# A four-layer graph network on one core: pair 0's layer 2 in another place, matrix quarters summed by adding transfers, and layer 2 of the last two pairs as two sweeps

## The chip, the core and the metric

The kernel runs on one core of one Trainium2 chip. Its engines are TensorE (PE, matrix products), VectorE (DVE), ScalarE (ACT), GpSimd (POOL, here used to issue transfers) and SyncE (SP, which issues transfers only). Each works through its own queue in order and meets the others at semaphores. The metric is the device time of one launch in microseconds, lower is better; of several runs the median counts.

## What is computed

Eight batches of 2048 nodes with 64 features pass through four layers. Every layer ends in a residual sum and a layer norm over the 64 features, and every layer multiplies with the same 2048 x 2048 matrix `adj` (f32):

```python
# layer 0: a graph convolution of order 3 with weights of each node's own
As = [I, A, 2*A@A - I];  w = einsum('nd,dkio->nkio', embedding, weight)
x = layernorm(x + einsum('bnki,nkio->bno', x_g, w) + b)       # x_g: As applied to x
# layer 1: attention over the nodes where adj > 0.5
e = leaky(s1[:, :, None] + s2[:, None, :]);  att = softmax(where(adj > 0.5, e, -9e15))
x = layernorm(x + elu(att @ x))
# layer 2
x = layernorm(x + (adj + I) @ (x @ W.T + b) / deg)
# layer 3: three steps, with row 0 of v replaced at the start
for _ in range(3):
    effects = adj @ v;  v = relu([v, effects] @ W1.T + b1) @ W2.T + b2
x = layernorm(x + v)
```

## The kernel before

**Tiling.** Two batches of 64 features make one *pair* of 128 columns, so there are four pairs, 0 to 3. The state of a pair is a slot `SX0` to `SX3` of 128 partitions x 16 tiles x 128 (1 MB). Three more slots exist: `SA`, `SB` and `SH`. The transposed matrix is read again for each product, in tiles of 256 x 512 f32 (512 KB) by SP (`fetch`, line 234) into a ring of six buffers. A *sweep* (line 1074) multiplies one or two slots with the whole matrix: four column chunks of 512, for each eight tiles, for each tile two matmuls of 128x512 per slot. The sums collect in `acc` (two PSUM banks), and an evicting helper takes them from there.

**Layers.** Layer 0 needs two sweeps per pair (`first_product`, `second_product`) and then, for each of 16 node tiles, eight matmuls into `yp` (line 601) that ACT multiplies with the embedding (line 624) and DVE adds up (636, 638). During the first sweep masks of the matrix are written to DRAM by column, and later by row. Layer 1 is work of DVE and ACT: `scores` (line 700) finds row maxima (line 731), `weights` (798) makes the exponentials in four passes (DVE 809, ACT 817, DVE 822, ACT 825) that PE then multiplies (836), and `finish` (853) normalises; its second `pf` product (870) and the norm after it end a pair's layer 1 (`x2`). Layer 2 is one sweep with `adj + I`, whose diagonal tiles lie in `a_plus_i`; `z_evict` (942), `layer2_tail` (977) and `start_chunk` (1001) take each chunk through a linear map, a norm and a transpose. Layer 3 is three sweeps per pair, each started by a seed product (line 1082) and followed by `h_evict` (951) and `u_chunk` (1024) or, in the last step, `last_chunk` (1044) and `store`.

**The last two pairs.** For pairs 2 and 3 together (`JOINT`), layer 3 takes the matrix in four quarters and the two pairs' columns in four blocks, and forms the product from seven quarter products in place of eight (`joint_layer3`, line 1247). For that it needs four sums and differences of quarters, `s1` to `s4`. These are made in `joint_layer2` (1188): it reads each tile once for both pairs, and `sums` (1170) adds the tiles on DVE (line 1172) and stores them from POOL (1174); diagonal tiles are read a second time without the added identity (`pure`, 1152). The block sums of the two pairs are made by `sums_of_u` (1322), and `keep_m1`, `seed_c22` and `combine` put the quarter products together.

**What sets the order.** `Plan` (line 38) writes the whole order by hand when the program is built: helpers are generators that say which engine they want and what they wait for, with a cost for each step; a number (rank) given to `plan.start` breaks ties. The long chain of sweeps is one such generator (`sweeps`, 1404) with rank 1000, so that anything else that is ready goes in between. PE's order around the change was: all sweeps of layer 0, ending with `second_product(3)`; then for pairs 0 and 1 layer 2 and the three sweeps of layer 3; then the joint part. Tails of layers 2 and 3 run from one queue (`tails`, 971), which begins when layer 0 of the last pair is done.

Of the kernel before, what the change touches and what calls it, by code (L numbers as in the profile page):

```python
# [17 lines left out]
P = 128  # L18
# [125 lines left out]
def resnorm_d4_kernel(  # L144
# [69 lines left out]

    SX = [slots.tile([P, NT, P], F32, name=f"SX{p}") for p in range(NPAIR)]
# [111 lines left out]
    for e in range(2):  # L327
# [20 lines left out]
        for m in ("s1", "s2", "s3", "s4")  # L348
# [84 lines left out]
    def row_tile(t, an, k, done):  # L433
        yield "ACT", [done]
        dg = tiny([P, 1], "dg", 2)
        nc.scalar.activation(an, an, AF.Copy, accum_out=dg)
        done = plan.run("ACT", act(N) + 0.2, done)
        yield "DVE", [done, mr_ring]
        nc.vector.tensor_scalar_add(dg, dg, 1.0)
        nc.vector.reciprocal(rdeg[:, t : t + 1], dg)  # L440
        mk, km = mr_ring.take([P, N], "mr", BF16)
        nc.vector.tensor_scalar(mk, an, THRESHOLD, NEG_INF, ALU.is_le, ALU.mult)
        done = plan.run("DVE", 1.13 + 0.26, done)
        bc_ring.give(k, done)
        nc.gpsimd.dma_start(by_row[t], mk)
        done = plan.dma("DMA", 512, done)
        mr_ring.give(km, done)
        at["by_row", t] = done
        if all(("by_row", i) in at for i in range(NT)):
            at["rows"] = done  # L450
# [125 lines left out]
    def second_pass():  # L576

        for n in range(NPAIR * NCH):
# [32 lines left out]
            xg_ring.give(kx, t_pe)  # L611

# [46 lines left out]
    def layer1(p):  # L659
# [38 lines left out]
        plan.start(10 + p, scores(p, sv, xc, s_rows, done))  # L698

    def scores(p, sv, xc, s_rows, done):  # L700
        s2b = []
        for e in range(2):
            yield "DMA", [bc_ring, done, "rows"]
# [228 lines left out]
    JOINT = (NPAIR - 2, NPAIR - 1)  # L932
    SH_of = {p: SH for p in range(NPAIR)}

    def after_l2(p):
        return SB if p == 0 else SX[p - 1] if p < NPAIR - 1 else SX[0]

    def u_of(p, s):

        return SX[p] if s == 1 else SB if p == NPAIR - 1 else SA  # L940

    def z_evict(p, c, pa, give, done):
# [4 lines left out]
        give(done)  # L947
# [23 lines left out]
    def tails():  # L971
        yield "PE", [("x1", NPAIR - 1)]
# [28 lines left out]
    def start_chunk(p, c, v, done):  # L1001
# [10 lines left out]
        yield "PE", [done, pp_ring]  # L1012
# [11 lines left out]
    def u_chunk(p, c, w, dst, bias, s, done):  # L1024
        yield "PE", [done, pp_ring]
# [48 lines left out]
    def sweep(*products, masks=False):  # L1074

        for c in range(NCH):
            pas = []
            for source, evict, need, before, seed in products:
                yield "PE", [acc_ring, *before(c)]
                pas.append(acc_ring.take([P, CW], "acc"))  # L1080
                if seed:
                    nc.tensor.matmul(  # L1082
                        pas[-1][0], lhsT=seed, rhs=SH[:, tiles(c), :], start=True, stop=False
# [44 lines left out]

    RQ = AQ // 2

    def quarters(k, r):

        return [(k, r), (k, r + RQ), (k + 2, r), (k + 2, r + RQ)]

    def order_of_joint():
        for k in range(2):
            for r in range(RQ):
                order_of_a.extend((c, q, True) for c, q in quarters(k, r))
        for s in range(3):
            for m in ("a11", "a12", "s2", "s3", "a22", "s1", "s4"):  # L1140
                i, j = {"a11": (0, 0), "a12": (0, 1), "a22": (1, 1)}.get(m, (0, 0))
                for k in range(2):
                    for r in range(RQ):
                        if m[0] == "a":
                            order_of_a.append((k + 2 * i, r + RQ * j, False))
# [3 lines left out]
    def pure(k, r):  # L1149

        yield "SP", [("group", k, r), *([xg_ring] if len(xg_ring.freed) > 1 else [NEVER])]
        got = []
        for c, q in (quarters(k, r)[i] for i in (0, 3)):
            t, kt = xg_ring.take([P, 2, CW], "pure")
            nc.sync.dma_start(t, tile_of_adj(c, q))
            got.append((t, kt, plan.dma("SP", 512, xg_ring.t)))
        return got

    def sums(k, r, taken):

        tiles4 = [(t, kt, got) for t, kt, got, _ in taken]
        own = {}
        if r // 2 == k:
            own = dict(zip((0, 3), (yield from pure(k, r))))
        a11, a12, a21, a22 = ((own.get(i) or tiles4[i])[0] for i in range(4))
        ready = [(own.get(i) or tiles4[i])[2] for i in range(4)]

        def out_of(m, a, b, op, *after):
            yield "DVE", [bc_ring, *after]
            t, kt = bc_ring.take([P, 2, HALF], m)  # L1170
            t = t.rearrange("p a b -> p (a b)")[:, 0 : 2 * CW].rearrange("p (t n) -> p t n", n=CW)
            nc.vector.tensor_tensor(t, a, b, op)
            done = plan.run("DVE", dve(2 * CW), *after)
            nc.gpsimd.dma_start(sum_tiles[m][k, r], t)  # L1174
            bc_ring.give(kt, plan.dma("DMA", 512, done))
            return t, done

        s3, d3 = yield from out_of("s3", a11, a21, ALU.subtract, ready[0], ready[2])
        s1, d1 = yield from out_of("s1", a21, a22, ALU.add, ready[2], ready[3])
        s2, d2 = yield from out_of("s2", s1, a11, ALU.subtract, d1)  # L1180
        s4, d4 = yield from out_of("s4", a12, s2, ALU.subtract, d2)
        for (_, kt, _, free), d in zip(taken, (d2, d4, d1, d1)):
            a_ring.give(kt, max(free, d))
        for _, kt, _ in own.values():
            xg_ring.give(kt, d2)
        refill()

    def joint_layer2():
        p, o = JOINT
        at["group", 0, 0] = 0.0  # L1190
        for k in range(2):
            pas = {}
            for r in range(RQ):
                taken = []
                for i, (c, q) in enumerate(quarters(k, r)):
                    n = next(used)
                    if r == 0 and i in (0, 2):
                        if i == 0:
                            yield "PE", [po_ring, ("x2", p), ("x2", o)]
                            t2, kp = po_ring.take([P, 2, CW], "po")  # L1200
                            pas[c] = [(t2[:, e, :], kp) for e in range(2)]
                        else:
                            pas[c] = []
                            for e in range(2):
                                yield "PE", [acc_ring]
                                pas[c].append(acc_ring.take([P, CW], "acc"))
                    for e, pair in enumerate(JOINT):
                        yield "PE", [("a", n)]
                        t, kt = a_tiles[n]
                        for b in range(2):  # L1210
                            m = 2 * q + b
                            nc.tensor.matmul(
                                pas[c][e][0],
                                lhsT=SX[pair][:, m, :],
                                rhs=t[:, b, :],
                                start=(r == 0 and i in (0, 2) and b == 0),
                                stop=(r == RQ - 1 and i in (1, 3) and b == 1),
                            )
                        done = plan.run("PE", mm(CW, 2), ("a", n))
                        if r == RQ - 1 and i in (1, 3):  # L1220
                            if i == 3:
                                give = lambda t, kk=pas[c][e][1]: acc_ring.give(kk, t)
                            else:
                                give = give_half(pas[c][e][1])
                            plan.start(1, z_evict(pair, c, pas[c][e][0], give, done))
                    del a_tiles[n]
                    taken.append((t, kt, at["a", n], done))
                    if i == 0:
                        nxt = (k, r + 1) if r + 1 < RQ else (k + 1, 0)
                        at[("group", *nxt)] = plan.free["PE"]  # L1230
                    spent[0] += 1
                plan.start(5, sums(k, r, taken))
                refill()

    halves_left = {}

    def give_half(kp):
        def give(t):
            left, last = halves_left.pop(kp, (2, 0.0))
            if left == 1:  # L1240
                po_ring.give(kp, max(t, last))
            else:
                halves_left[kp] = (1, max(t, last))

        return give

    def joint_layer3():
        p, o = JOINT
        U, _ = e_ring.take([P, 2, HALF], "u23")
        T12, _ = e_ring.take([P, 2, HALF], "t12")  # L1250
        T34, _ = e_ring.take([P, 2, HALF], "t34")
        T = [
            t[:, i, :].rearrange("p (t n) -> p t n", n=P) for t in (T12, T34) for i in range(2)
        ]
        for s in range(3):
            up, uo = u_of(p, s), u_of(o, s)
            B11, B21, B12, B22 = up[:, 0:8], up[:, 8:16], uo[:, 0:8], uo[:, 8:16]
            plan.start(0, sums_of_u(s, T, B11, B21, B12, B22))
            u = lambda pair, half: lambda k: ("u", pair, s, 2 * half + k)
            t = lambda i: lambda k: ("t", s, i, k)  # L1260
            seed = gv if s else w31v
            held = {}

            for m, B, need, evict, seeded in (
                ("m1", B11, u(p, 0), None, None),
                ("m2", B21, u(p, 1), None, (p, 0)),
                ("m6", T[1], t(1), "u2", None),
                ("m7", T[2], t(2), "u3", None),
# [209 lines left out]
```

## Time and profile before

| what | before |
|---|---|
| median of 3 runs | 2132.62 us (2131.99 to 2137.06) |
| the profiled execution | 2133.99 us |
| its span | 2132.2 us |
| granted TensorE clock, mean | 0.994 |
| PE, matmuls busy | 2067.3 us (97%) |
| DVE busy | 1496.4 us (70%) |
| ACT busy | 974.9 us (46%) |
| POOL busy | 213.0 us (10%) |
| moved by transfers | 495.85 MB, 233 GB/s on average |

The profile is one execution, taken by the hardware. A row of the timeline gives the start and the length in us, the engine, the line, the operation, what it writes and reads, and the count; the time in brackets is how long the engine stood idle before it, and what ended that. Matmuls of f32 with 512 columns appear as two records each, so that x16 stands for eight matmuls. A row of the windows table gives a stretch of the span with the busy time in it, the granted clock, the mean busy share of the 16 DMA engines and the rate.

### The profile page before, as it was taken

The page shows a single profiled execution, that of the slowest core. Times are in us where ns is not written, and L with a number is a line of the kernel's source. Part 1 is how long each engine was busy: PE and PEld are TensorE (multiplying, and loading weights), DVE is VectorE, ACT ScalarE, POOL GpSimd, SP SyncE. Part 2 cuts the span into 40 slices and gives each one's busy share as a digit, 9 for nine tenths or more (in the row PEclk, how much of TensorE's full clock was granted, in tenths as well). Part 3 has the DMA queues.
Part 4 walks back from the last instruction along what each step waited for, and adds up shares of the span by engine and source line. Part 5 has one row for each costly group of instructions (what it writes and reads, how often), then busy time and mean ns, then how long its engine had stood idle before and what let it go on. Part 6 is the DMA issues. An engine that isn't in the chain of part 4 may idle for free. (4 is left out here: it accounts for less than half of the span.)

```text
span 2132.2 us, 19037 instructions
## 1 busy us (share of the span) xinstructions
PE 2067.3 (97%) x6325; PEld 914.9 (43%) x6325; DVE 1496.4 (70%) x1908; ACT 974.9 (46%) x1794; POOL 213.0 (10%) x374
## 2 busy tenths in 40 slices
PE   8999999999999999999798999989999999999998
PEld 3444444433433443433343453443444444444444
DVE  2226647998799999789998979999796455120214
ACT  0025424567776566777624857336575012000002
POOL 2310000100110100000010101011010110000000
PEclk9999999999999999999899999999999999999999
DMA  9799835634443465554388778897776777878785
GB/s 303 267 333 345 306 105 209 218 122 136 138 137 131 159 238 169 170 178 150 124 309 299 254 267 285 279 339 239 264 236 234 290 255 273 280 254 281 251 288 188
DMA packets 208740, 495.85 MB, mean 233 GB/s; under 512 B 20274, under 2 KB 28594, under 8 KB 204530
## 3 DMA queue, kind: packets, MB, share of 16 engines
q1 hardware_dynamic: 165058, 347.62, 48.0%
q0 software_dynamic: 39360, 144.92, 19.7%
q10 hardware_dynamic: 4224, 2.10, 0.4%
q8 instruction: 50, 0.82, 0.2%
q14 instruction: 48, 0.39, 0.1%
HBM read 446.14 MB, written 46.33 MB: 231 GB/s over the span
## 5 line engine op out<-in xcount | busy, mean ns | idle before, releaser
L1093 PE MATMUL acc<-a,SX 128*128 128x512 f32 x1024 | 465.8, 598 | 9.6 <-DMA SX<-in_x 6.6
L1093 PE MATMUL acc<-a,SA 128*128 128x512 f32 x768 | 348.6, 596 | 13.1 <-DMA a<-in_adj_t 12.4
L817 ACT ACTIVATE e<-e,sv 128x1024 f32<-128x1024 f32 x256 | 280.1, 1154 | 114.4 <-DVE e L809 110.6
L731 DVE CUSTOM_DVE_ANT_0 junk<-s2b,mr 128x2048 bf16<-128x2048 f32 x128 | 292.7, 2287 | 5.2 <-DMA mr<-by_row 3.9
L624 ACT ACTIVATE terms<-yp,emb_sb 128x128 f32<-128x128 f32 x896 | 243.5, 400 | 113.6 <-PE yp L601 113.3
L1093 PEld LDWEIGHTS acc<-a,SX 128*128 128x128 f32 x1024 | 190.3, 191 | 242.2 <-issue 229.6
L822 DVE TENSOR_TENSOR e<-e,mb 128x2048 f32<-128x2048 f32 x128 | 290.0, 2286 | 6.0 <-ACT e L817 5.4
L809 DVE TENSOR_TENSOR e<-s1b,mk 128x2048 f32<-128x2048 f32 x128 | 289.1, 2286 | 6.5 <-PE po L836 4.0
L825 ACT ACTIVATE e<-e 128x2048 f32<-128x2048 f32 x128 | 245.0, 1928 | 67.5 <-DVE e L822 67.2
L601 PE MATMUL yp<-SH,xgT 128*128 128x512 f32 x512 | 246.9, 607 | 3.3 <-ACT sv L358 3.3
L836 PE MATMUL po<-e,SX 128*64 128x512 f32 x1024 | 235.4, 602 | 3.1 <-ACT e L825 3.1
L1093 PEld LDWEIGHTS acc<-a,SA 128*128 128x128 f32 x768 | 140.9, 190 | 186.0 <-issue 166.0
L1299 PE MATMUL acc<-a,t 128*128 128x512 f32 x384 | 168.7, 592 | 0.0
L636 DVE TENSOR_TENSOR terms<-terms 128x512 f32<-128x512 f32 (+1 forms) x176 | 130.0, 738 | 42.2 <-ACT terms L624 38.2
L601 PEld LDWEIGHTS yp<-SH,xgT 128*128 128x128 f32 x512 | 90.9, 189 | 145.7 <-issue 137.6
L836 PEld LDWEIGHTS po<-e,SX 128*64 128x64 f32 x1024 | 68.1, 137 | 155.8 <-issue 133.7
L601 PE MATMUL yp<-SH,y2T 64*128 64x512 f32 x512 | 128.3, 617 | 0.0
L804 POOL DMA_DIRECT2D mk<-by_col x128 | 69.0, 540 | 546.7 <-DVE e L809 452.1
L1093 PE MATMUL acc<-a,SB 128*128 128x512 f32 x256 | 118.3, 595 | 0.0
L1299 PEld LDWEIGHTS acc<-a,t 128*128 128x128 f32 x384 | 72.0, 190 | 86.1 <-issue 86.1
L601 PEld LDWEIGHTS yp<-SH,y2T 64*128 64x128 f32 x512 | 43.6, 186 | 79.9 <-issue 76.4
L1093 PEld LDWEIGHTS acc<-a,SB 128*128 128x128 f32 x256 | 47.2, 190 | 57.3 <-issue 57.3
(225 smaller groups left out, 1677.7 us busy)
## 6 DMA issues: line engine op xcount, KB each, us to landing
a<-in_adj_t SPq DMA_DIRECT2D x496, 512.0 KB, 5.5
a<-s SPq DMA_DIRECT2D x96, 512.0 KB, 4.5
mr<-by_row POOLq DMA_DIRECT2D x64, 512.0 KB, 5.9
mk<-by_col POOLq DMA_DIRECT2D x128, 256.0 KB, 5.0
an<-in_adj SPq DMA_DIRECT2D x16, 1024.0 KB, 10.7
s<-s POOLq DMA_DIRECT2D x32, 512.0 KB, 5.0
a<-a_plus_i SPq DMA_DIRECT2D x24, 512.0 KB, 5.0
by_col<-mk POOLq DMA_DIRECT2D x32, 256.0 KB, 5.8
```

What stands on the lines that cost most here:

```text
L601: nc.tensor.matmul(yp[:, e, :], lhsT=y2T[rows, cs] if k2 else xg[:, e, cs], rhs=(wk2 if k2 else w01)[rows, hs], start=(k2 == h), stop=(k2 ...
L624: nc.scalar.activation(batches(terms[0][:, dd, :]), term, AF.Copy, scale=weight)
L636: nc.vector.tensor_tensor(a, a, b, ALU.add)
L731: nc.vector.tensor_tensor_reduce(out=junk, in0=s2b[e][0], in1=masks[t][0], scale=1.0, scalar=LOWEST, op0=ALU.add, op1=ALU.max, accum_out=m ...
L804: nc.gpsimd.dma_start(mk, by_col[jt // 2][:, jt % 2, h * HALF : (h + 1) * HALF])
L809: nc.vector.tensor_tensor(e, s1b[0], mk.unsqueeze(1).to_broadcast([P, 2, HALF]), ALU.add)
L817: nc.scalar.activation(e[:, i, :], e[:, i, :], AF.Prelu, bias=sv[:, 2 + i, jt : jt + 1], alpha=ALPHA)
L822: nc.vector.tensor_tensor(e, e, mb[0], ALU.add)
L825: nc.scalar.activation(e, e, AF.Exp)
L836: nc.tensor.matmul(po[i * C : (i + 1) * C, f, :], lhsT=SX[p][:, t, i * C : (i + 1) * C], rhs=e[:, i, f * CW : (f + 1) * CW], start=(t == 0 ...
L1093: nc.tensor.matmul(pa, lhsT=source[:, m, :], rhs=t[:, i, :], start=(m == 0 and not seed), stop=(m == NT - 1),)
L1299: nc.tensor.matmul(pa, lhsT=B[:, 2 * r + b, :], rhs=at_[:, b, :], start=(r == 0 and b == 0 and not go_on), stop=(r == RQ - 1 and b == 1), ...
```

## The change

It has three parts, and buffers move to other slots with them.

1. Layer 2 of pair 0 is swept ahead of layer 0's last pass (`second_product(3)`). For that, pair 0 uses other slots: its transposed state goes into `SX0` (as soon as the sweep has used it, "x1 used"), its layer-2 result into `SA`, its u into `SB` (after the last pass, "y1 used") and `SH` (after layer 0's weights, "w0 used"). Tails no longer wait for layer 0 of the last pair. `scores` of pair 0 gets rank 1.2 in place of 10 and no longer waits until all row masks are written; the other pairs' get 9.5 + p.
2. The four sums of quarters are made by 64 transfers from DRAM to DRAM, issued by POOL: for each of 4 x 8 tiles one copy and one that adds to it. They are due every 14 us from 320 us of the plan on. Block sums and the putting together of the seven products are reordered to suit the new sums.
3. `joint_layer2` and what belonged to it go. Pairs 2 and 3 get one sweep of layer 2 each, pair 2 first.

```diff
-        plan.start(10 + p, scores(p, sv, xc, s_rows, done))
+        plan.start(1.2 if p == 0 else 9.5 + p, scores(p, sv, xc, s_rows, done))
...
-            yield "DMA", [bc_ring, done, "rows"]
+            yield "DMA", [bc_ring, done]
...
-    JOINT = (NPAIR - 2, NPAIR - 1)
-    SH_of = {p: SH for p in range(NPAIR)}
+    JOINT = (NPAIR - 1, NPAIR - 2)
+    SH_of = {p: SH if p else SX[0] for p in range(NPAIR)}
...
-        return SB if p == 0 else SX[p - 1] if p < NPAIR - 1 else SX[0]
+        return SA if p == 0 else SX[p - 1] if p < NPAIR - 1 else SX[0]
...
-        return SX[p] if s == 1 else SB if p == NPAIR - 1 else SA
+        if s == 1:
+            return SX[p] if p else SH
+        return SB if p in (0, 1, NPAIR - 1) else SA
...
     def tails():
-        yield "PE", [("x1", NPAIR - 1)]
...
-        yield "PE", [done, pp_ring]
+        yield "PE", [done, pp_ring, *(["x1 used"] if p == 0 else [])]
...
+        room = {0: ["y1 used"], 1: ["w0 used"]}.get(s, []) if p == 0 else []
+        yield "PE", [done, pp_ring, *room]
...
+    def sums_of_a():
+        n = itertools.count()
+        for m, a, b in (
+            ("sa", "a12", "a22"),
+            ("sb", "a11", "a12"),
+            ("sc", "sa", "a11"),
+            ("sd", "sc", "a21"),
+        ):
+            for x in (a, b):
+                for k, r in sum_tiles[m]:
...
+                    yield "DMA", [320.0 + 14.0 * next(n), *before]
+                    nc.gpsimd.dma_start(
+                        sum_tiles[m][k, r], part, **({"accum_op": ALU.add} if x == b else {})
+                    )
+                    done = plan.dma("DMA", 900 if x == b else 512) + 1.0
...
-            for m in ("a11", "a12", "s2", "s3", "a22", "s1", "s4"):
+            for m in ("sb", "a11", "sc", "sd", "a21", "a22", "sa"):
...
+            def keep(s, k, pa, done):
+                yield "ACT", [done]
+                nc.scalar.copy(half(X, k), pa)
+            def x_of(s, k, pa, ka, done):
+                nc.vector.tensor_tensor(half(X, k), pa, half(X, k), ALU.subtract)
+            def z_and_v(s, k, pa, ka, done):
+                nc.vector.tensor_tensor(half(Z, k), half(X, k), pa, ALU.subtract)
+                seeded(p, 2 + k, pa, False)
+                nc.vector.tensor_tensor(half(V, k), pa, half(X, k), ALU.subtract)
...
             products = [second_product(p)]
             if 0 < p < NPAIR - 1:
                 products.append(first_product(p + 1))
+            if p == NPAIR - 1:
+                yield from sweep(layer2_product(0))
+                at["x1 used"] = 0.0
             yield from sweep(*products)
+        at["y1 used"] = 0.0
         for p in range(NPAIR - 2):
-            yield from sweep(layer2_product(p))
+            if p:
+                yield from sweep(layer2_product(p))
             for s in range(3):
                 yield from sweep(layer3_product(p, s))
+        yield from sweep(layer2_product(NPAIR - 2))
...
-        yield from joint_layer2()
+        yield from sweep(layer2_product(NPAIR - 1))
         yield from joint_layer3()
...
     plan.start(1, rows_of_adj())
+    plan.start(1, sums_of_a())
     plan.start(1, stacks())
```

## The prediction

> **What bounds the kernel now.** I read the page first for the totals, then the timeline of PE for every wait it has, then the windows table for the transfers beside it.
>
> ```profile
> span 2132.2 us, 19037 instructions
> PE 2067.3 (97%) x6325; PEld 914.9 (43%) x6325; DVE 1496.4 (70%) x1908; ACT 974.9 (46%) x1794; POOL 213.0 (10%) x374
> DMA  9799835634443465554388778897776777878785
> ```
>
> PE is busy 2067.3 of 2132.2 us, so all that an edit can win without removing matmuls is the 64.9 us in which PE stands still. The timeline of PE shows where they are; an entry in brackets is the idle time before the row and what ended it. The two groups that this change touches:
>
> ```profile
> 1005.82 7.13 PE L1093 MATMUL acc<-a,SX 128*128 128x512 f32 x16 [3.07 <-ACT z L945]
> ...
> 1026.55 1.94 PE L836 MATMUL po<-e,SX 128*64 128x512 f32 x8 [1.08 <-ACT e L825]
> ...
> 1033.36 1.13 PE L981 MATMUL ps_emb<-w2bd,z 128*128 128x128 f32 x8 [2.89 <-DVE SB L990]
> 1035.12 2.04 PE L981 MATMUL ps_emb<-w2bd,z 128*128 128x128 f32 x8 [0.64 <-DVE SB L990]
> 1044.58 0.48 PE L1015 MATMUL ps_vT<-ident,v 128*128 128x128 f32 x1 [7.42 <-DVE v L1007]
> ...
> 1120.43 1.98 PE L1093 MATMUL acc<-a,SA 128*128 128x512 f32 x4 [1.24 <-DMA a<-in_adj_t]
> 1124.71 1.98 PE L1093 MATMUL acc<-a,SA 128*128 128x512 f32 x4 [2.30 <-DMA a<-in_adj_t]
> 1128.37 3.70 PE L1093 MATMUL acc<-a,SA 128*128 128x512 f32 x8 [1.68 <-DMA a<-in_adj_t]
> ...
> 1723.24 0.66 PE L1015 MATMUL ps_vT<-ident,SX 128*128 128x128 f32 x4 [1.59 <-DVE SX L510]
> 1727.28 0.63 PE L1015 MATMUL ps_vT<-ident,SX 128*128 128x128 f32 x4 [1.54 <-DVE SX L510]
> ```
>
> Group one is pair 0's layer 2: its tail (linear map, norm, transpose) runs on DVE and ACT, layer 0 and the sweeps have nothing left for PE, and it waits 3.07 + 1.08 + 2.89 + 0.64 + 7.42 = 15.1 us. Group two is the same tail for the two last pairs at once; with its smaller entries (0.66, 0.68, 0.67, 0.67, 0.31, 0.35, 1.33, 0.88) it comes to 8.7 us between 1687 and 1797. Between them lie 5.2 us for adjacency tiles at 1120. The rest is not touched: 6.6 at the start, 6.4 up to 300, 2.5 up to 1000, 3.0 near 1150, 6.6 near 1404 to 1430, 10.1 at the end.
>
> The windows table shows how much transfer PE stands beside it (time, PE busy with count, clock, share of the 16 DMA engines, GB/s):
>
> ```profile
> 1110.00:1160.00 50.00, 41.76 (x120) 1.00 0.92 339
> 1240.00:1330.00 90.00, 90.00 (x293) 1.00 0.84 293
> 1400.00:1440.00 40.00, 33.35 (x96) 1.00 0.99 355
> ```
>
> At a share of 0.84 PE never waits; at 0.92 and 0.99 it does. So the bound is PE's own work, and DMA is what can open holes in it.
>
> **Part 1: PE's work itself.** Layer 2 of the last pairs goes from 32 tiles used twice to two sweeps of 32: 128 matmuls both times. The seven quarter products and their seeds are 112 and 8 per step both times. PE's 2067.3 us stay.
>
> **Part 2: pair 0's layer 2 moved ahead of the last pass.** In the changed order its 64 matmuls stand right behind the second pf of pair 0 and three layer-0 tiles (yp; a fourth stands just ahead of that pf), and its tail lies beside the last pass of layer 0 (64 matmuls of 0.86 us and 16 yp tiles of 5.1), which doesn't need it. The 15.1 us go. What is late next is the input of the moved sweep, x2 of pair 0:
>
> ```profile
> 749.65 1.05 PE L870 MATMUL pf<-back,poT 128*128 128x130 f32 x8
> ...
> 773.05 0.69 DVE L510 TENSOR_TENSOR SX<-SX,ln_r 128x512 f32<-128x512 f32 x1
> ```
>
> Before, that norm ends at 773.7 with DVE never idle from 734.0. The changed order has some 2.9 us less on DVE in this stretch (the sum of its rows), so about 770.8. PE's order up to the first pf is the same; from there (731.2) to the sweep it has 34.5 us of work, so it arrives at 765.7 and waits 5 us; the wait is the sweep's first matmul, and all of PE's queue stands behind it. From below, 0, if DVE drops more; from above 12, since the four yp tiles now stand back to back and each needs 16 x 0.400 = 6.4 us of ACT (row L624) for 5.1 of PE, with two buffers. I take 6, near the DVE row. In the sweep itself PE has only po to fill, and po waits for weights from DVE, four passes of 2.29 us per eight matmuls with scores between; in the trace such waits total 3.1 us. Between 0 and 8, taken as 1.5.
>
> The DMA waits of 5.2 us at 1120 arose where pair 0's first layer-3 sweep ran bare, at 0.86 us a matmul, beside two 1 MB broadcasts. In the new order that sweep is mixed with yp tiles, and reads half as fast. I take 4 of 5.2 as gone (0 to 5.2).
>
> **Part 3: the last pairs apart.** Pair 2's tail now lies under pair 3's sweep, pair 3's under the first four quarter products, which need only pair 2's u (27 us by 32 matmuls of 0.86). The 8.7 us go, 1 stays for short waits as in the row at 1404 (0.44 to 0.67). The cover is the 55 us sweep; without it the 8.7 would return. The price is 32 more tiles: 64 in about 125 us are 268 GB/s, and PE stood 276 without a wait:
>
> ```profile
> 1800.00:1900.00 100.00, 100.00 (x275) 47.67 (x274) 16.40 (x26) 5.57 (x8) 0.00 (x0) 1.00 0.82 276
> ```
>
> So 0. DVE's 32 adds of 1.22 us (39 us), 32 stores and 8 second loads fall away after 1650, where DVE is under 60% busy: 0. Two more sums of u per step and one combine less per half are about 4 us of DVE in all, at 17% busy: 0. The bank that is kept for two products waits for a DVE add of 0.69 us under 6.9 us of matmuls: 0.
>
> **Part 4: the sums by transfers.** 64 transfers of 512 KB on POOL's queue, due every 14 us from 320 on: 32 copies and 32 that add. Their issue is 64 x 0.54 to 0.74 us on a POOL that is 10% busy; behind them stand the mask loads (mr, mk), three buffers deep, and DVE waits for those. For a plain 512 KB the queue table gives 144.92 MB for 19.7% of 16 engines' span, so 1.52 us of all engines. No adding transfer is in the trace. POOL's 10% alone would say that the whole costs nothing. The Trainium skill speaks against that (DMA: Bandwidth & Descriptors, "Issuing engines are not separate DMA queues"): transfers from POOL run on the same 16 engines as SP's. The rows at 0.92 and 0.99 bear it out, and what decides is where the 64 fall. Up to about 770 the share is 0.37 to 0.64, and there they are hidden. In the moved sweep (0.83 by the same mix later, in pair 1's) it is mostly copies: 0.83 + 1.52/14 = 0.94, just at the edge. The last 8 adds fall into pair 0's layer-3 steps at 0.84, where 14 us leave 0.16 x 14 = 2.2 us. If an add costs like the copy row, 0 is lost. The Trainium skill (Collectives: The Full Stack, "The bandwidth ceiling: the fold count and why AG ≠ RS ≠ AR") has an add read two sources and run at half a copy's rate: an estimated 3.0 us, 0.8 over, times 8 = 7. No run here shows which. I take 3.5 of 0 to 7; a gain is excluded, since the traffic is additional.
>
> **The sum.** 2134.0 (the profiled execution: span 2132.2 and 1.8 around it) - 15.1 - 8.7 - 4.0 + 6.0 + 1.5 + 1.0 + 3.5 = 2118.2. The median of the runs lies 1.4 under the profiled execution, so 2117.
>
> **Rivals.** *Better covered*: x2 arrives in time and the adds cost no more than copies; 2117 - 6 - 3.5 - 1.5 = 2106. For it: DVE ran 39 us there without a pause and its order is free to favour the norm. Against: ACT's 6.4 us per yp tile. *Given back at the moved sweep*: the wait for x2 takes 12, po 8, nothing is won at 1120, the adds cost 7: 2117 + 6 + 6.5 + 4 + 3.5 = 2137 at most, 2129 if only the first two hit. For it: DVE is 84 to 98% busy from 700 on, and PE's queue is in order. *Slower, by the adds*: one mechanism, the adding transfer at several times a copy. It decides from where 8 x (T - 2.2) outweighs the 15.8 us won and 6.4 more, T = 5.0 us, 3.3 copies. At T = 6 the last 8 cost 30 us, and the other 24 hold mask loads in the same queue beyond their slack of some 3.5 us (three buffers of 4.7 us, less one in use, against 5.9 us to landing), of which I count 6 on PE: 2117 + 30 + 6 - 3.5 = 2150. Against it: most adds fall in half-idle stretches, and rule and row both say 1.5 to 3. *That it doesn't do what it says* would be pair 0's sweep behind the last pass; the changed order shows it ahead.
>
> **How the numbers follow.** Forecast 0.52, better covered 0.20, given back 0.16, slower 0.12. A measurement of this kernel tells about 0.3% (6.4 us) from no change. Faster (below 2126) holds the first two and a little of the third: 0.74; the rest of the third is "same", 0.14; slower 0.12. The range: down to 2103, just under "better covered"; up to 2134, the middle of "given back", leaving out its end and "slower".
>
> **What would show it.** Right: on PE's timeline no wait over 1 us at ps_emb or ps_vT of pair 0, nor between layer 2 and the quarter products; one wait of about 6 us before the moved sweep, ended by DVE SX L509; PE busy 2065 to 2070; DMA share near 0.95 in the moved sweep and in pair 0's layer 3. Wrong: PE rows there ended by DMA a<-in_adj_t beyond 10 us in total (adds dear), or DVE idle for mr or mk, or po waiting for ACT e L825 beyond 10 us.

## The result, and the profile after

The changed kernel took 2118.22 us (median of 4 runs, 2112.12 to 2120.24), the kernel before beside it 2132.3 us. The ratio is 0.9917 [0.9898, 0.9935], 0.8% faster. The profiled execution of after, 2112.12 us, is the quickest of its four; a second profile of the same kernel, called *after again* below, has a span of 2119.3 us and stands for the median better. Where the two differ, both are given.

The head of the page of after, and the digits of DMA:

```profile
span 2110.3 us, 19036 instructions
PE 2064.0 (98%) x6325; PEld 914.9 (43%) x6325; DVE 1462.1 (69%) x1879; ACT 980.7 (46%) x1791; POOL 253.5 (12%) x406
DMA  9799837775456578788659979788776777778885
```

The span is 21.9 us shorter with the same 6325 matmul records. PE stands still for 46.3 us in place of 64.9; the other 3.3 us are PE's own busy time, which the prediction had taken as fixed (the last section shows what moves it between executions). The timeline of PE in after, with its larger waits behind 300 us (time, length, ..., idle before and what ended it):

```profile
474.38 1.94 PE L836 MATMUL po<-e,SX 128*64 128x512 f32 x8 [1.35 <-ACT e L825]
477.98 0.63 PE L671 MATMUL ps_xT<-ident,SX 128*128 128x128 f32 x4 [1.66 <-DVE SX L509]
...
688.61 0.66 PE L563 MATMUL ps_xg<-ident,SX 128*128 128x128 f32 x4 [3.49 <-ACT terms L624]
...
757.89 0.66 PE L530 MATMUL ps_y<-ident,y1T 128*128 128x128 f32 x4 [1.38 <-ACT terms L624]
...
777.53 15.62 PE L1097 MATMUL acc<-a,SX 128*128 128x512 f32 x36
...
1123.60 1.98 PE L1097 MATMUL acc<-a,SH 128*128 128x512 f32 x4 [1.26 <-DMA a<-in_adj_t]
1127.98 1.98 PE L1097 MATMUL acc<-a,SH 128*128 128x512 f32 x4 [2.40 <-DMA a<-in_adj_t]
1130.99 5.42 PE L1097 MATMUL acc<-a,SH 128*128 128x512 f32 x12 [1.03 <-DMA a<-in_adj_t]
...
1426.60 3.46 PE L1097 MATMUL acc<-a,SB 128*128 128x512 f32 x4 [1.98 <-DMA a<-in_adj_t]
```

Groups one and two are gone, without a rest. The moved sweep starts at 777.53 with no wait. The waits for adjacency tiles near 1120 are still there. And there are waits that before did not have, at 474 to 478 and 677 to 689. The windows of after (PE busy, clock, DMA share, GB/s) at the moved sweep, at 1120, at pair 0's later layer-3 sweeps and in the joint part:

```profile
770.00:850.00 80.00, 79.14 (x245) 1.00 0.78 271
1110.00:1140.00 30.00, 24.97 (x75) 1.00 1.05 339
1240.00:1330.00 90.00, 90.00 (x310) 1.00 0.90 319
1800.00:1900.00 100.00, 100.00 (x276) 1.00 0.80 266
```

At 0.90 PE does not wait; at 1.05 it does. (A share near 1 is not enough by itself: *every7* below passes 1110 to 1140 at 1.02 with PE busy for all 30 us.) The moved sweep shows 0.78, not the 0.95 foretold.

### The profile page after: what moved, and what is told of

It is laid out like the page before. It is cut to its first block, busy times and chain, and to the rows that moved or that the text cites. A ratio compares the mean times of both kernels' runs of the same rounds, so it can differ in the third digit from the quotient of the medians.

```text
span 2110.3 us, 19036 instructions
## 1 busy us (share of the span) xinstructions
PE 2064.0 (98%) x6325; PEld 914.9 (43%) x6325; DVE 1462.1 (69%) x1879; ACT 980.7 (46%) x1791; POOL 253.5 (12%) x406
## 4 chain that ended last, share of the span: by engine, by line
PE 61%; issue 24%; DVE 8%; DMA 3%; ACT 2%; POOL 0%; SPq 0%; POOLq 0%; ACTq 0%; DVEq 0%
PE acc L1097 35%; PE yp L600 12%; PE po L836 10%; DVE junk L731 3%; DMA a<-in_adj_t 2%; DVE terms L636 2%; DVE e L822 1%; DVE e L809 1%; PE ps_u L1032 1%; ACT terms L624 1%; PE acc L1086 1%; DMA an<-in_adj 1%; ACT e L817 1%; PE pf L870 1%; PE ps_sv L681 0%
## 5 line engine op out<-in xcount | busy, mean ns | idle before, releaser
L1097 PE MATMUL acc<-a,SX 128*128 128x512 f32 x1152 | 519.7, 597 | 6.5 <-DMA SX<-in_x 6.5
L1097 PE MATMUL acc<-a,SB 128*128 128x512 f32 x768 | 352.0, 598 | 4.8 <-DMA a<-in_adj_t 4.1
L1097 PEld LDWEIGHTS acc<-a,SX 128*128 128x128 f32 x1152 | 214.6, 191 | 266.0 <-issue 258.1
L1097 PEld LDWEIGHTS acc<-a,SB 128*128 128x128 f32 x768 | 140.8, 190 | 178.5 <-issue 168.1
L636 DVE TENSOR_TENSOR terms<-terms 128x512 f32<-128x512 f32 (+1 forms) x176 | 129.9, 738 | 49.7 <-ACT terms L624 45.5
L1097 PE MATMUL acc<-a,SA 128*128 128x512 f32 x256 | 119.5, 600 | 2.5 <-DMA a<-in_adj_t 2.5
L1210 PE MATMUL acc<-a,t 128*128 128x512 f32 x192 | 85.4, 592 | 0.0
L490 ACT ACTIVATE ln_sq<-SX 128x512 f32<-128x512 f32 x48 | 30.6, 638 | 94.0 <-DVE SX L995 38.9
L718 POOL DMA_DIRECT2D mr<-by_row x64 | 34.8, 549 | 315.0 <-DVE mx L731 268.8
## 6 DMA issues: line engine op xcount, KB each, us to landing
an<-in_adj SPq DMA_DIRECT2D x16, 1024.0 KB, 10.6
```

The lines of the kernel that those rows point to most:

```text
L636: nc.vector.tensor_tensor(a, a, b, ALU.add)
L1097: nc.tensor.matmul(pa, lhsT=source[:, m, :], rhs=t[:, i, :], start=(m == 0 and not seed), stop=(m == NT - 1),)
L1210: nc.tensor.matmul(pa, lhsT=B[:, 2 * r + b, :], rhs=at_[:, b, :], start=(start and r == 0 and b == 0), stop=(r == RQ - 1 and b == 1), skip ...
```

## The experiments

The theory after this profile: the two groups were worth what the waits said, the sums are nearly hidden, and the new early waits are the price. The rivals: the adding transfers eat a good part of the gain; or one part brings the whole of it. The kernels came in three batches of four: move_only to no_sums; joint_no_sums, old_ranks, every7 and after again; and the last four. The kernel before beside them had medians of 2134.9, 2134.8 and 2136.0 us, so kernels of different batches are compared by their ratios. The table gives for each the median, the ratio to the kernel before on the same chip, and from its one profile PE's busy time and the waits that PE's timeline shows, by stretch.

| kernel | median us | ratio [95%] | PE busy | waits 300 to 775 | 775 to 1000 | 1000 to 1160 | 1380 to 1450 | 1600 to 1820 |
|---|---|---|---|---|---|---|---|---|
| before | 2132.3 | 1 | 2067.3 | 2.8 | 0.2 | 23.3 | 6.6 | 8.7 |
| after | 2118.2 | 0.9917 [0.9898, 0.9935] | 2064.0 | 10.7 | 0.0 | 5.0 | 6.1 | 0.0 |
| after again | 2117.9 | 0.9917 [0.9902, 0.9931] | 2071.7 | 9.8 | 0.8 | 4.5 | 7.0 | 0.0 |
| move_only | 2130.1 | 0.9975 [0.9966, 0.9984] | 2071.2 | 4.9 | 7.1 | 0.9 | 8.3 | 11.8 |
| joint_only | 2133.2 | 0.9996 [0.9985, 1.0006] | 2070.7 | 0.0 | 3.6 | 25.0 | 4.7 | 0.0 |
| adds_as_copies | 2113.7 | 0.9901 [0.9887, 0.9916] | 2067.2 | 10.7 | 0.0 | 2.5 | 6.1 | 0.0 |
| no_sums | 2115.9 | 0.9913 [0.9900, 0.9926] | 2068.6 | 4.8 | 7.2 | 0.8 | 6.9 | 0.0 |
| joint_no_sums | 2125.3 | 0.9955 [0.9943, 0.9968] | 2066.8 | 2.8 | 0.2 | 23.2 | 5.2 | 0.0 |
| old_ranks | 2101.2 | 0.9845 [0.9830, 0.9860] | 2062.4 | 1.7 | 0.0 | 2.9 | 9.0 | 0.0 |
| every7 | 2114.4 | 0.9905 [0.9890, 0.9919] | 2066.6 | 5.9 | 3.2 | 0.0 | 13.6 | 0.0 |
| move_old_ranks | 2125.3 | 0.9945 [0.9932, 0.9958] | 2072.0 | 5.4 | 0.6 | 0.8 | 7.7 | 15.5 |
| before_new_rank | 2139.9 | 1.0018 [1.0011, 1.0026] | 2077.3 | 2.9 | 0.0 | 6.4 | 7.5 | 23.7 |
| old_ranks_every7 | 2112.8 | 0.9891 [0.9878, 0.9904] | 2067.7 | 1.3 | 2.5 | 7.8 | 7.1 | 0.0 |
| old_ranks_every10 | 2105.4 | 0.9853 [0.9840, 0.9866] | 2064.3 | 1.7 | 1.1 | 4.6 | 8.2 | 0.0 |

### One part at a time

*move_only* is before with pair 0's layer 2 moved, its slots and the new rank; *joint_only* is after with pair 0 where it was, in its old slots and with the old ranks.

```diff
 move_only, from before:
+            if p == NPAIR - 1:
+                yield from sweep(layer2_product(0))
+                at["x1 used"] = 0.0
             yield from sweep(*products)
...
-        plan.start(10 + p, scores(p, sv, xc, s_rows, done))
+        plan.start(1.2 if p == 0 else 9.5 + p, scores(p, sv, xc, s_rows, done))
 joint_only, from after: the same lines back, the sums and the two sweeps kept
```

> Pair 0's layer 2 moved ahead, with its slots and the scores' ranks, while the last two pairs keep their shared sweep and the sums on DVE. Theory M (each part removes its own waits and pays its own price): the 15.1 us at ps_emb and ps_vT of pair 0 go, 3 to 8 us come back as waits for ACT and DVE before the moved sweep, so 2121 us (2117 to 2125), and the 8.7 us between 1687 and 1797 of before are still there. Theory S (the scores' new ranks cost, the transfers don't): new waits of some 8 us between 470 and 770, as in the changed kernel, show here too. Theory R (the sums' transfers cost): no such waits before 700 here, and 2117 or less.

> The sums by adding transfers, the new order of the seven products and two separate sweeps for the last pairs, while pair 0's layer 2 stays behind the last pass, with the old slots and ranks. Theory M: the 8.7 us near the last pairs' layer 2 go, the 15.1 us of pair 0 stay, the transfers cost 0 to 4, so 2126 us (2123 to 2129). Theory R: the transfers cost 8 us or more, through loads of masks and of adjacency tiles that come late, so 2132 or above, no gain.

Each part removes its group (the 15.1 us at 1000 to 1090 in the one, the 8.7 us of the last pairs in the other), and yet they bring 0.25% and nothing that the measurement tells from zero; together 0.83%. So each part alone pays its gain back elsewhere. Where joint_only pays is on PE's timeline, in pair 0's layer-3 sweeps:

```profile
1121.29 1.99 PE L1095 MATMUL acc<-a,SA 128*128 128x512 f32 x4 [1.21 <-DMA a<-in_adj_t]
1126.16 2.41 PE L1095 MATMUL acc<-a,SA 128*128 128x512 f32 x4 [2.88 <-DMA a<-in_adj_t]
1129.99 6.13 PE L1095 MATMUL acc<-a,SA 128*128 128x512 f32 x8 [1.42 <-DMA a<-in_adj_t]
...
1145.30 1.98 PE L1095 MATMUL acc<-a,SX 128*128 128x512 f32 x4 [1.99 <-DMA a<-in_adj_t]
1149.27 1.13 PE L1095 MATMUL acc<-a,SX 128*128 128x512 f32 x2 [1.98 <-DMA a<-in_adj_t]
```

Over the whole span it waits 19.1 us for adjacency tiles (before 13.1), 13.8 of them between 1100 and 1300 (before 5.2). Four adds are issued right there, at 1105.9, 1119.6, 1132.7 and 1137.1. They are the obvious suspect.

### The sums

*adds_as_copies* lets the 32 adding transfers copy, *no_sums* and *joint_no_sums* leave all 64 out and read plain quarters (from after and from joint_only).

```diff
 adds_as_copies:
-    sum_tiles[m][k, r], part, **({"accum_op": ALU.add} if x == b else {})
+    sum_tiles[m][k, r], part, **{}
 no_sums, joint_no_sums:
-    plan.start(1, sums_of_a())
...
-            src = sum_tiles[c][q]
+            src = tile_of_adj(*q)
```

> The changed kernel with the 32 adding transfers as plain copies of the same bytes to the same place: the addition of the second quarter is left out, so the products of the last two pairs in layer 3 are other numbers. The order of every queue is that of the changed kernel. If an add costs like a copy: within 1 us of the changed kernel (2118). If it costs twice a copy, as I sized it: 2 to 4 us less, with the waits for adjacency tiles at 1120 shorter. Rival (adds several times a copy): 8 us less or more. POOL's issue of an add falls from 1.1 us to 0.7.

> The changed kernel without any of the 64 transfers: in place of the four sums, plain quarters of the matrix are read, so the products of the last two pairs in layer 3 are other numbers; the number of tiles read is the same. Theory M with transfers that are nearly hidden: 2113 to 2116, since 3.5 us were counted for them. Theory R: 2108 or less, and the waits between 470 and 700 and those for tiles at 1120 are gone. Theory S: the waits between 470 and 700 stay.

> Parts 2 and 3 as in the kernel joint_only (pair 0's layer 2 behind layer 0's last pass, last pairs' layer 2 as two sweeps), but the 64 summing transfers are left out and the seven products read plain quarters, so the sums are missing from the result. Theory: alone, the joint part won its 8.7 us and gave them back as waits for adjacency tiles (19.1 us against 12.4 before), because the last sums fell beside pair 0's layer-3 sweeps that had no yp tiles among them. Then without the transfers: waits for adjacency tiles back to 12 us or less, group two still gone, group one still there, time 2134.9 - 8 = 2126 to 2128, a ratio of 0.996 to 0.997. Rival: the transfers are innocent and the pair of sweeps itself costs what it wins (its order or a slower clock): ratio 0.9985 to 1.0005 as in joint_only.

What an add costs can be read from the queue table (packets, MB, share of 16 engines' span), first after, then adds_as_copies:

```profile
q0 software_dynamic: 46272, 161.70, 25.0%
```

```profile
q0 software_dynamic: 42176, 161.70, 22.4%
```

The same bytes take 0.250 x 2110.3 = 527.6 us in place of 0.224 x 2109.6 = 472.6 us of all engines: 55 us for 32 adds, 1.72 us each on top of the copy's 1.52 (the 64 copies against no_sums' 17.7% give 1.54). An add thus costs about 3.2 us where the prediction's estimate was 3.0. On the time, adds as copies are some 3.4 us quicker (0.9901 against 0.9917), but the intervals of the ratios overlap. The same order without any sum is not to be had: with the transfers away the plan writes another order (a wait of 4.57 us at 789.51 that move_only has too and after has not), so that no_sums, at 0.9913, says only that the sums do not cost much.

joint_no_sums against joint_only shows a clear difference: 0.9955 against 0.9996, intervals apart, 8 to 9 us, with 5.1 us of waits for adjacency tiles between 1100 and 1300 in place of 13.8. The windows of joint_only and of joint_no_sums at pair 0's first layer-3 sweeps:

```profile
1110.00:1160.00 50.00, 38.92 (x100) 0.93 1.01 334
```

```profile
1110.00:1160.00 50.00, 41.86 (x120) 1.00 0.93 337
```

So without the sums the joint part wins its group two (9.6 us by joint_no_sums), and with them it gives it back. That the transfers do this, and not the other order that comes with them (joint_no_sums has before's waits again up to 1160), is argued from the four adds beside the waits; joint_only with its adds as copies was not run. In after the first layer-3 sweep of pair 0 has yp tiles among it, and 5.0 us of such waits are left of the 13.8. That is one half of why the parts bring more together than apart.

### The rank of scores

The waits at 474 to 478 and at 677 to 689 belong to no part of the prediction's sum. *old_ranks* restores the old ranks and the wait for the row masks. Of this edit only one number counts: with 10 + p for pairs 1 to 3, or with the wait, the program that the plan writes is the same as after's byte for byte, so all of the difference comes from pair 0's 1.2 in place of 10:

```diff
-        plan.start(1.2 if p == 0 else 9.5 + p, scores(p, sv, xc, s_rows, done))
+        plan.start(10 + p, scores(p, sv, xc, s_rows, done))
...
-            yield "DMA", [bc_ring, done]
+            yield "DMA", [bc_ring, done, *(("by_row", i) for i in range(NT))]
```

> The changed kernel with the old ranks of scores (10 + p for every pair) and the old wait for all row masks. It tells whether the new short waits of about 8 us in all between 470 and 690 us come from pair 0's scores being preferred. If the ranks make them: those waits fall to some 2.5 us as before, but x2 of pair 0 comes later, so the wait at the moved sweep grows; time between 2112 and 2118. If the early rank is what makes x2 punctual: the moved sweep waits 10 us or more at its first matmuls and the time is 2122 to 2130. If the order hardly changes: 2117 to 2119 and the same short waits.

It is the quickest kernel of the study, below all three cases of the expectation: 2101.2 us, 0.9845 [0.983, 0.986], 17 us under after again, which ran beside it. The early waits are gone but for one of 1.68 us at 749, as its windows with PE's busy time show (first old_ranks, then after):

```profile
475.00:500.00 25.00, 25.00 (x80) 1.00 0.67 176
675.00:700.00 25.00, 25.00 (x81) 1.00 0.60 156
```

```profile
475.00:500.00 25.00, 23.12 (x86) 1.00 0.46 113
675.00:700.00 25.00, 20.42 (x68) 0.93 0.59 159
```

I had feared that without the early rank the moved sweep would wait for x2. It does not: it starts at 768.82, 8.7 us sooner than in after, with no wait. What PE stood for at 688.61 in after was the multiplication of a yp tile on ACT, behind three passes of weights (the timeline of ACT in after):

```profile
679.90 1.91 ACT L825 ACTIVATE e<-e 128x2048 f32<-128x2048 f32 x1 [2.52 <-DVE e L822]
682.10 4.39 ACT L817 ACTIVATE e<-e,sv 128x1024 f32<-128x1024 f32 x4 [0.29 <-DVE e L809]
686.40 2.16 ACT L624 ACTIVATE terms<-yp,emb_sb 128x128 f32<-128x128 f32 x8
```

ACT itself had waited 2.52 us for DVE. The rank thus shifts work between DVE's and ACT's queues, and PE pays where layer-1 passes fall ahead of layer 0's. The early waits need the sums in the plan as well: between 300 and 700 us the kernels with the new rank but without sums (move_only, no_sums, before_new_rank) have 2.9 us, like before (2.8), and joint_only, with sums and the old rank, has none. The cost of the adds is not the reason: as copies in the same order they leave the 7.8 us as they are. That points to the order. Two further kernels put the rank on and off elsewhere: *move_old_ranks* is move_only with the old rank, *before_new_rank* is before with the new rank alone.

> The kernel move_only with the old ranks of scores: only pair 0's layer 2 moves, with its slots. If the new rank is what ate the gain of the move in move_only (2130 us, where the 15.1 us of group one were gone): the waits near 476, 687, 753 and 791 us are gone and the time is 2113 to 2118, a ratio of 0.990 to 0.992. If the move itself is worth little, whatever the rank: 2126 to 2131. Whether the last pairs' waits of 8 us near 1698 to 1793 stay: both say yes.

> The kernel before with one edit, the new rank of scores (1.2 for pair 0, 9.5 + p for the others). If the rank by itself makes the short waits between 470 and 790 us and slows the clock behind them: 10 to 17 us slower than before, 2145 to 2152, a ratio of 1.004 to 1.008, and PE waits over 1 us near 475, 680 and 690. If it hurts only together with the moved sweep: 0.998 to 1.002. If an earlier x2 helps pair 0's layer 2 where it stood: a ratio under 0.998.

The rank costs in each of the three comparisons, in two of them less than expected: 0.9975 against 0.9945 for the move alone, 0.9917 against 0.9845 for the whole, and 1.0018 [1.0011, 1.0026] for before, which lies in the range of the case that it hurts only together with the moved sweep. The place differs. In before_new_rank group one is gone too (2.0 us left of 15.1), and 23.7 us of waits stand at 1600 to 1820 instead, 12 of them for the last pair's layer 1. move_old_ranks (2125.3 us) lies between its two cases, and neither names what it shows, a new wait in the old joint layer 2:

```profile
1645.91 3.37 PE L1215 MATMUL po<-a,SX 128*128 128x512 f32 x4 [4.26 <-DVE SX L510]
1679.91 8.59 PE L1215 MATMUL acc<-a,SX 128*128 128x512 f32 x16 [3.16 <-DMA a<-in_adj_t]
```

PE, ahead by the move, comes to the joint layer 2 before x2 of pair 3 is ready: a sweep for both pairs at once needs both inputs at its start, while two sweeps need the second one 55 us later. That is the other half of the gain from both parts together. With the old ranks throughout, the four kernels are 1, 0.9945 (move), 0.9996 (joint), 0.9845 (both): parts 0.6% in sum, both 1.55%, 20 us more. In the one profile of each the spans give 2132.2 - 2125.9 - 2130.5 + 2100.8 = -23.4 us. The waits on PE's timeline make up 56.2 - 45.2 - 49.7 + 28.5 = -10.2 of it. Most of the rest is the clock: half of the time in which PE was busy at half clock (up to 2090 us) is 4.8 us in before, 11.3 in move_old_ranks, 9.1 in joint_only and 5.0 in old_ranks, so -10.6.

### When the sums run

*every7* (from after), *old_ranks_every7* and *old_ranks_every10* (from old_ranks) issue the sums every 7 or 10 us.

```diff
-                    yield "DMA", [320.0 + 14.0 * next(n), *before]
+                    yield "DMA", [320.0 + 7.0 * next(n), *before]
```

> The changed kernel with the 64 summing transfers due every 7 us in place of 14, so that they end near 800 us, before the moved sweep, in the stretch with a DMA share of 0.4 to 0.65. If the sums cost their time only where they meet the layer-3 sweeps: no or 1 to 2 us of waits for adjacency tiles near 1120 in place of 5.0, time 2113 to 2116. Rival: twice as dense in POOL's queue they hold back the mask loads (mr, mk) and DVE, x2 comes later: wait at the moved sweep of 5 us or more, time 2120 to 2128. Rival: the waits near 1120 belong to the two broadcasts and stage stores there, not to the sums: 2117 to 2119 with 3 to 5 us still there.

> The kernel old_ranks with the summing transfers due every 7 us in place of 14. In every7 the waits for adjacency tiles near 1120 fell from 5.0 us to none. If the two edits add up: 2101.2 - 3 = 2097 to 2100, no wait near 1110. If the denser transfers shift the written order so that other short waits appear (every7 had new ones of 4.6, 2.0 and 1.8 us): 2101 to 2108.

> The kernel old_ranks with the transfers due every 10 us, ending near 960 us, in the middle of the moved sweep. If what matters is that none falls beside pair 0's layer-3 sweeps: as with every 7 us, 2097 to 2101. If what matters is that none falls in the moved sweep either: slower than every 7 us by 1 to 3 us. If the order written by the plan is what decides, the two differ in either direction by up to 8 us for no reason that the DMA share shows.

Every 7 us the last add is issued at 764 and none meets the moved sweep or layer 3. In every7 the waits near 1120 are indeed gone, as its first case said, but 7.5 us more stand at 1380 to 1450 (4.6 of them one wait for a transpose's input), and the gain over after (0.9905 against 0.9917) is inside the intervals. On old_ranks it is a loss (0.9891 for 0.9845, some 10 us), against the first case of the expectation and beyond the second; every 10 us (0.9853) is not told apart from every 14, and is 7 us quicker than every 7, where two of its cases had it equal or slower. That leaves the third, the order that the plan writes. In old_ranks_every7 adjacency waits stand near 1130 although no sum is near; POOL's timeline of old_ranks_every7 shows what is, two broadcasts of 1 MB, and PE's timeline of the same kernel the waits behind them:

```profile
1117.68 0.71 POOL L769 DMA_DIRECT2D s1b<-s_rows  x1
1118.38 0.56 POOL L769 DMA_DIRECT2D mb<-m_rows  x1
```

```profile
1129.11 1.98 PE L1097 MATMUL acc<-a,SH 128*128 128x512 f32 x4 [1.07 <-DMA a<-in_adj_t]
1133.52 1.98 PE L1097 MATMUL acc<-a,SH 128*128 128x512 f32 x4 [1.54 <-DMA a<-in_adj_t]
1137.07 1.98 PE L1097 MATMUL acc<-a,SH 128*128 128x512 f32 x4 [1.57 <-DMA a<-in_adj_t]
```

The same pair comes 10 to 20 us ahead of the waits in after (issued at 1103 and 1412; waits from 1123 and 1426) and in old_ranks (1401; from 1413). In every7 the pair at 1106 passes without a wait, and in move_only the pair at 1098. In both no sum is near, and the last yp tile ends only 3 to 4 us ahead of the pair; in old_ranks_every7 it ends nearly 50 us ahead. By these kernels, broadcasts on a sweep that has long run without other work can open a hole alone; shortly after yp tiles, as in after too (the last one ends at 1098.5, the pair comes at 1103), it took the sums beside them: 5.0 us in after, 2.5 with its adds as copies, none in every7, whose order is a little different.

### The same kernel twice

> The changed kernel once more, on the chip of the three others and in as many rounds, as the measure for them: 2118 us, ratio 0.990 to 0.9935. Its profile tells which of the short waits and which of the PE busy time (2064.0 us in the first profile, 2067 to 2071 in the others) are the same in another execution: if the busy time is the kernel's own it is 2064 again, if it varies with the execution it lies anywhere from 2064 to 2071.

The median is the same (2117.93 us), but the two profiled executions differ by 9.0 us, of which 7.7 are PE's busy time with the same instructions. The windows of 25 us in which the clock differs, first in after, then in after again (PE busy, clock, DMA share, GB/s); at 675 and at 1425 both show 0.93:

```profile
250.00:275.00 25.00, 24.08 (x75) 1.00 0.72 256
475.00:500.00 25.00, 23.12 (x86) 1.00 0.46 113
1125.00:1150.00 25.00, 21.23 (x62) 1.00 1.06 349
```

```profile
250.00:275.00 25.00, 22.76 (x63) 0.86 0.70 250
475.00:500.00 25.00, 21.79 (x80) 0.93 0.49 117
1125.00:1150.00 25.00, 20.48 (x56) 0.86 1.06 350
```

The clock dips at waits, in steps of 0.07, and in after again five steps more. A step is 3.41 us at half clock, at most 1.71 us lost of 25. Over both profiles, half of the time in which PE was busy at half clock is 5.0 us in after and 11.9 in after again: 6.9 of the 7.7.

## Why the prediction was right, point by point

The time was right (2118.2 for 2117), and so was the mechanism of the two large terms: the **15.1 us** of group one and the **8.7 us** of group two left the timeline, and the 1 us kept back for the latter did not come. The terms around them were less good, and that their errors cancelled is luck.

- **Part 1, PE's 2067.3 us stay.** The records stay, the time does not: 2062.4 to 2077.3 us over the profiles of the study, and 2064.0 and 2071.7 for after, both outside the 2065 to 2070 named as a sign. The 64.9 us of standing still were therefore not "all that an edit can win": before ran at half clock for 13.65 us from 1035 on, in group one, with PE busy for 6.2 of them, so that some 3.1 us more were to be won there.
- **Wait for x2, 6 us (0 to 12).** The size was too large and its cause another. PE waits 2.9 us ahead of the sweep, at the four yp tiles that stand back to back, for ACT (the row at 757.89), which the step had named as the upper bound's reason. That bound was too high because 0.400 us is the mean length of records that overlap: the sixteen of a yp tile take ACT 4.3 us, not 6.4 (row below), against some 5.5 of PE (742.38 to 747.93 in before). The last norm of x2 ends at 779.5, later than the 770.8 worked out, but the sweep's first tiles do not need it. From there to 1000 us, where the wait for po (1.5) was to be, stand 0 to 0.8 us.
- **4 of 5.2 us at 1120 gone.** This failed: 5.0 us remain in after, 4.5 in after again. The step took the yp tiles in the first layer-3 sweep as the cure. That sweep does pass without a wait, but the broadcasts at 1103 fall on its end, behind the last yp tile, and the waits stand in the second sweep, which runs bare. Without sums beside it that sweep passes too (move_only has no such wait there). So what stands here is in part the price of the sums, 2.5 us of it that of adding; with the 3.5 for the adds, put into the same steps, the forecast was 4.7 there, near the 5.0. The waits of 1.72 and 1.03 us at 1147 and 1157, which I had counted as untouched, went instead.
- **The adds, 3.5 us (0 to 7).** Some 3.4 us by the ratios of after and adds_as_copies, though the intervals overlap. The estimate from half a copy's rate was near (3.2 us an add for 3.0), and the rival with its bound at T = 5.0 us is refuted by that size.
- **Not in the sum: the rank of scores.** The step took x2's time from the changed order but did not ask what the new rank does to DVE and ACT before that. With the sums in the plan it brings 7.8 us of waits between 300 and 700 (before 2.8). Taking it back wins 17 us on the median, more than the whole change brings. Of the profiles' difference, after again is 18.5 us longer than old_ranks, 9.0 in waits and 9.3 in PE's busy time (6.9 of them by the half clock); after is 9.5 us longer, 8.0 of it in waits. With the old rank the time is 2101, below the range (2103 to 2134) and below the "better covered" rival (2106), for another reason than that gave.
- **A slip without effect.** The waits of before between 300 and 1000 are 3.0 us, not 2.5.

The row of ACT that sets the second point right is from the timeline of before:

```profile
745.97 4.34 ACT L624 ACTIVATE terms<-yp,emb_sb 128x128 f32<-128x128 f32 x16
```

So the time came out right by terms that cancelled. The forecast had 15.8 us less of waits; PE's timeline has 19.7 less in after and 18.7 in after again. In after, x2, po and the last pairs took back 2.7 us for the 8.5 forecast and the waits at 1147 and 1157 gave 3.0, while the rank took 5.0. PE's busy time, which had no term, is 3.3 us shorter than before's in after and 4.4 longer in after again. With the old rank the forecast would have been 16 us too high. "Given back at the moved sweep" did not happen, and the transfers' share there was 0.78.

Three things stay open: why the 1.2 of pair 0 and the sums make the early waits only together; how much of the 13.8 us in joint_only is the transfers and how much the order; and the part of PE's busy time that the half clock does not explain.

## What to carry to other kernels

Two parts of a change can be worth nothing apart and 1.5% together, when each removes the place where the other gives its gain back; try them together, and each with the small edits beside it undone, before judging either. A change of priority among helpers is a change of its own: here one number cost more than the whole change brought. And where an order is written by a plan, a kernel with one step less is another order, so take away the cost (an add turned into a copy), not the step.

## What the runs showed of the hardware

**A short wait of PE can cost more than its length.** In after again PE stood 3.91 us at 252, and the four records behind it took 3.78 us; in after it stood 2.88 us and they took 1.98, the usual time:

```profile
252.24 3.78 PE L600 MATMUL yp<-SH,xgT 128*128 128x512 f32 x4 [3.91 <-ACT sv L359]
```

```profile
250.92 1.98 PE L600 MATMUL yp<-SH,xgT 128*128 128x512 f32 x4 [2.88 <-ACT sv L359]
```

The granted clock shows why. It falls to half for 3.41 us at a time (twice that at 250), and the falls start on a fixed grid: in after again at 250.49, 482.60, 694.22, 1131.13 and 1434.92 us, which are 68, 62, 128 and 89 steps of 3.413 us apart. What decides is, by the count below, how long PE stands still within one window of this grid, and the grid lies differently in each execution. In both profiles PE has the same waits of 1.3, 1.7 and 0.2 us near 480. In after the window holding most of them leaves PE 1.75 us busy, and the next keeps its clock; in after again it leaves 1.54, and the next has half:

```profile
474.65:478.06 3.41, 1.75 (x9) 1.00 0.29 111
478.06:481.48 3.42, 3.20 (x12) 1.00 0.00 0
```

```profile
479.19:482.60 3.41, 1.54 (x10) 1.00 0.09 34
482.60:486.01 3.41, 3.41 (x4) 0.50 0.18 40
```

The same count over the 14 profiles, from 20 to 2090 us, and for windows that began at full clock: in 40 of them PE stood 1.87 us or more, and all 40 were followed by half the clock; of 12 between 1.70 and 1.86 us two were; of the rest none, but for one at 548 us in old_ranks_every7 and one near 76 us in every profile, which its waits do not explain. The Trainium skill (TensorE: Matmul & The Clock Gate, "What's actually happening") states a free-running window of about 3.4 us, with half the clock after at least one idle window. The window, its grid and the half are what these traces show; the window need not be idle throughout, since some 1.9 us of it were enough.

A window at half clock costs up to 1.71 us, as much as PE had to do in it. Half of the time in which PE was busy at half clock is 4.8 to 15.0 us in the 14 profiles. Taken off, PE's busy times of 2062.4 to 2077.3 us become 2057.0 to 2062.9. A gain in waits is thus worth up to 1.71 us more for each window in which PE no longer stands about half the time; the 3.3 us between before and after are not of this kind (4.8 and 5.0 us).

**An adding transfer from DRAM to DRAM** took some 3.2 us of all 16 engines for 512 KB, a copy 1.5, and landed after 10 us where the same transfer as a copy took 7 (issue table, the sum sd: 10.5 and 7.2 us; for sc 9.7 and 8.2). POOL spent 1.1 us on issuing one, and 0.5 on a copy between DRAM buffers.
